# SyncE's transfers in written order, the maxima's split ahead of GpSimd's additions, and an opening with filters beside the loading of x

## The chip, the cores and the metric

The kernel runs on one core of one Trainium2 chip. Its time is device microseconds of that core; a verdict rests on the median of several executions. One execution was recorded by the hardware profiler, and the numbers that are read from a trace belong to that one. The engines are named as the profile names them: PE (TensorE), PEld (its weight loads), DVE (VectorE), ACT (ScalarE), POOL (GpSimd) and SP (SyncE, which issues transfers and computes nothing).

## What is computed

A block of a transformer on x of shape 4 x 2048 x 512, all in float32: a layer norm, then x + attention + a layer of experts. Attention has 16 heads of 32; queries and keys pass through a filter in the frequency domain, which is linear over the 32 numbers of a head and can therefore be multiplied into the weights. Cut to what matters:

```python
xn = _layernorm(x)                      # over 512, no scale or offset
q, k, v = split(xn @ w_qkv)             # 16 heads of 32
mask = sigmoid(mask_logits)
q = irfft(rfft(q) * mask); k = irfft(rfft(k) * mask)
attn = softmax(q k^T / sqrt(32))        # 2048 x 2048 for each of 4 x 16
attention = (attn v) @ w_out + b_out
best = argmax(softmax(xn @ w_gate))     # top 1 of 8 experts
# the first 100 tokens of each expert, in order of tokens, get
# gate * (xn @ w_expert + b_expert); all other tokens get 0
out = x + attention + experts
```

## The kernel before

**Groups, blocks and windows.** Four heads make a group; 4 sequences x 4 head groups make 16 groups `k`. A group has four blocks `n` of 512 queries. A block goes over the 2048 keys in 16 tiles `j` of 128 keys, two of them to a window, so a block has 8 windows, a group 32, and the program 512. In a window, for each tile and each pair of heads, TensorE first writes the negated row maxima into PSUM (`shift`, from the three bfloat16 rows of `negm`), adds the scores (`scores`), ScalarE takes the exponential into an `even` or `odd` tile, and one tile later TensorE multiplies with the values (`products`). For the sums of the softmax GpSimd adds each `odd` tile into its `even` one by an accumulating transfer (`pair`, line 834, 1 MB of traffic by the profile's count), and adds the `even` tiles up one window later (`add_to`).

**Maxima ahead of time.** The row maxima of a block are needed before its first exponential. A stream of items (`max_matmuls`, then `max_reduce` on VectorE) runs 40 items, that is ten windows, ahead. When a block is full, `max_negate` gives the negated maxima, and in the next window `max_close` (line 475) turns them with TensorE, ScalarE copies them out, GpSimd splits them into three bfloat16 rows, and SyncE sends these to `negm` (line 488).

**Closing a block.** `close_steps` (line 628) does, in windows after the block's end: 2 `fold` (row sums, to DRAM by SyncE, line 637), 3 `fetch` (back as 128 x 16, `few`, line 642), 4 `invert` (reciprocal on VectorE, and to DRAM), 5 `spread` (broadcast to `factor`), 7 `divide` on GpSimd (`ot`), 8 and 9 `result` (output projection, into `y`), 10 `add` (an accumulating transfer of 1 MB onto the output). The last block is closed by `close_last`, with a tile `y` read from the output before (line 888).

**Sequences.** While the third group of a sequence runs, the next sequence's x is loaded in four chunks (`load`, line 221), measured, given the bias and stored as the first sums of the output (`first_sums`, line 233); two chunks at a time fit. The chunks are loaded a second time, normalized and turned into `xnT` in the fourth group. `plan` (line 782) puts all such steps into windows: in the third group the loads of the four chunks at 11, 15, 19 and 23, the stores at 18, 22, 26 and 30, the second loads of the first two chunks at 30 and 31, the next weights (`load_qkv_weights`, line 381) at 31. The change of sequence is called a boundary here; there are three.

**What sets the order.** From line 724 on, TensorE, VectorE, ScalarE and GpSimd are wrapped in `InOrder`, which keeps the order in which the program writes their instructions. SyncE isn't wrapped: the framework's scheduler places its transfers where it expects them to be ready. Each engine then works its instructions off in that order, waiting for semaphores in place.

**The opening.** ScalarE issues the loads of the constants and of the weights (lines 128 to 181), SyncE those of x. The filter is made from the sigmoid (lines 182 to 188). For each of the four chunks of tokens the program measures, scales, normalizes and turns; after the first it filters group 0's weights (`filter_weights(0)`), writes them to DRAM (`wd`) and reads them back (`wg`). Two projections follow, then the first 40 items of maxima, with five further projections and the other three groups' filters between them. Then window 0 begins.

Of the kernel before, what the change touches and what calls it, by code (L numbers as in the profile page):

```python
# [22 lines left out]
H, DH = 16, 32  # L23
# [78 lines left out]
def attention_and_top1_experts(ctx: ExitStack, tc: tile.TileContext, a: dict, out: bass.AP):  # L102
# [24 lines left out]

    freq = const.tile([2 * NF, 2, P], F32, name="freq")
# [4 lines left out]
    falling = const.tile([P, E], F32, name="falling")  # L133
    nc.scalar.dma_start(out=falling, in_=a["c_falling"])
    token = const.tile([P, NT], F32, name="token")
    nc.scalar.dma_start(out=token, in_=a["c_token"])
    mask = const.tile([2 * NF, 1], F32, name="mask")
    logit_col = a["L0_attn_mask_logits"].rearrange("(f o) -> f o", o=1)
    nc.scalar.dma_start(out=mask[0:NF], in_=logit_col)
    nc.scalar.dma_start(out=mask[NF : 2 * NF], in_=logit_col)  # L140
# [30 lines left out]
    wd = [dram1.tile([P, NR, 3, P], F32, name=f"wd{c}") for c in range(NG)]  # L171
    raw = {}
    for s in range(2):
        for g in range(NR // 2):
            if g == 0:
                both = probs(s == 1)
            raw[s, g] = both[:, g]
            nc.scalar.dma_start(out=raw[s, g], in_=w_qkv[:, 2 * g : 2 * g + 2, s * DM : (s + 1) * DM])
    for c in range(NG):
        cols = slice(2 * DM + c * P, 2 * DM + (c + 1) * P)  # L180
        nc.scalar.dma_start(out=wd[c][:, :, 2, :], in_=w_qkv[:, :, cols])
# [9 lines left out]
    on = SimpleNamespace(tensor=nc.tensor, vector=nc.vector, scalar=nc.scalar, gpsimd=nc.gpsimd)  # L191
    def filter_weights(c):
        for s in range(2):
            pt, pw = bank(), bank()
            for r in range(NR):
                on.tensor.transpose(
                    pt[:, r * P : (r + 1) * P], raw[s, r // 2][:, r % 2, c * P : (c + 1) * P], ident
                )
            if s == 0:
                both = probs(c == 1)  # L200
            wt = both[:, s]
            on.scalar.copy(wt[:, 0, :], pt)
            for r in range(NR):
                at = slice(r * P, (r + 1) * P)
                on.tensor.matmul(pw[:, at], lhsT=wt[:, 0, at], rhs=filt, start=True, stop=True)
            on.scalar.copy(wt[:, 1, :], pw)
            nc.sync.dma_start(out=wd[c][:, :, s, :], in_=wt[:, 1, :].rearrange("p (r n) -> p r n", r=NR))
# [4 lines left out]
    def token_stage(b):  # L212
# [6 lines left out]
        def load(n, name="xs"):  # L219
            held[n] = chunk(name)  # L220
            nc.sync.dma_start(out=held[n], in_=x[b, n])
# [9 lines left out]
        def first_sums(n):  # L231

            nc.sync.dma_start(out=o[b, n], in_=held[n])

        def scale(first=0, last=NT):
            at = slice(first, last)
            on.scalar.activation(rstd[:, at], mv[:, at, 1], AF.Sqrt, bias=eps[:, 0:1])
            on.vector.reciprocal(rstd[:, at], rstd[:, at])
            on.gpsimd.tensor_tensor(shift[:, at], mv[:, at, 0], rstd[:, at], ALU.mult)
            on.gpsimd.tensor_scalar(shift[:, at], shift[:, at], -1.0, None, ALU.mult)  # L240
# [138 lines left out]
    wg, wo = {}, {}  # L379

    def load_qkv_weights(k):
        wg[k] = weights.tile([P, NR, 3, P], F32, name="wg", bufs=1)
        nc.sync.dma_start(out=wg[k], in_=wd[k % NG])

    def load_out_weights(k):
        c = k % NG
        wo[k] = weights.tile([P, DM], F32, name="wo")
        nc.sync.dma_start(out=wo[k], in_=a["L0_attn_w_out"][c * P : (c + 1) * P, :])
# [86 lines left out]
    def max_close(k, n):  # L475

        pn = bank()[0 : HG * TQ, 0:P]
        on.tensor.matmul(pn, lhsT=negs.pop((k, n)), rhs=ident, start=True, stop=True)
        rest = small.tile([HG * TQ, P], F32, name="rest")
        row = small.tile([HG * TQ, 3, P], BF16, name="row", bufs=2)  # L480
        on.scalar.copy(rest, pn)
        on.gpsimd.tensor_copy(row[:, 0, :], rest)
        for i in (1, 2):
            on.gpsimd.tensor_tensor(rest, rest, row[:, i - 1, :], ALU.subtract)
            on.gpsimd.tensor_copy(row[:, i, :], rest)
        negms[k, n] = qkv.tile([P, QB], BF16, tag="negm", name="negm", bufs=3)
        for i in range(3):
            nc.sync.dma_start(out=negms[k, n][i::DH, :], in_=row[:, i, :])
# [4 lines left out]
    def expert_steps():  # L493


        def begin():
            w_exp = chunk("w_exp")
            nc.sync.dma_start(out=w_exp, in_=a["L0_ffn_w_expert"].rearrange("(r p) n -> p r n", p=P))
            b_exp = work.tile([P, DM], F32, tag="b_exp", name="b_exp", bufs=1)
            nc.sync.dma_start(out=b_exp, in_=a["L0_ffn_b_expert"].partition_broadcast(P))  # L500
            entries = small.tile([P, NTAB, ST, 2], F32, name="entries")
            for i, table in enumerate(tables):
                nc.sync.dma_start(out=entries[:, i], in_=table.rearrange("(t p) c -> p t c", p=P))
# [124 lines left out]
    def close_steps(k, n, num, acc):  # L628
# [4 lines left out]
        def fold():  # L633
            den = work.tile([P, QB], F32, tag="den", name="den", bufs=1)
            on.scalar.copy(den, row_sums([acc]))
            held["sums"] = scratch.tile([HG, QB], F32, name="sums")
            nc.sync.dma_start(out=held["sums"], in_=den[0::DH, :])


        def fetch():  # L640
            held["few"] = small.tile([P, HG * QB // P], F32, name="few", bufs=2)
            nc.sync.dma_start(out=held["few"], in_=held["sums"].rearrange("h (c e) -> (h c) e", e=HG * QB // P))

        def invert():
            on.vector.reciprocal(held["few"], held["few"])
            held["inverse"] = scratch.tile([HG, QB], F32, name="inverse")
            nc.sync.dma_start(
                out=held["inverse"].rearrange("h (c e) -> (h c) e", e=HG * QB // P), in_=held["few"]
            )

        def spread():
            held["factor"] = work.tile([P, QB], F32, tag="factor", name="factor", bufs=1)
            for h in range(HG):
                nc.sync.dma_start(
                    out=held["factor"][DH * h : DH * (h + 1)], in_=held["inverse"][h].partition_broadcast(DH)
                )
# [12 lines left out]

        steps = [(2, fold), (3, fetch), (4, invert), (5, spread), (7, divide)]  # L670
        return steps + [(8, result, 0), (8, result, 1), (9, result, 2), (9, result, 3), (10, add)]

    def close_last(k, n, num, tiles, y):
# [9 lines left out]
        for t in range(TQ):  # L683
            on.vector.tensor_tensor(y[:, t, :], y[:, t, :], project(k, ot, t), ALU.add)
            if t % 2 == 1:
                nc.sync.dma_start(out=o[b, n, :, t - 1 : t + 1, :], in_=y[:, t - 1 : t + 1, :])
# [3 lines left out]
    for n in range(NQ):  # L690
        tiles = range(n * TQ, (n + 1) * TQ)
        load(n, "y" if n == 2 else "xs")
        for i in tiles:
            measure(i)
        scale(tiles[0], tiles[-1] + 1)
        for i in tiles:
            normalize(i)
            if i % 2 == 1:
                turn(i - 1)
        if n == 0:  # L700
            filter_weights(0)
            load_qkv_weights(0)
# [17 lines left out]
    first_projections = projections(0)  # L720
    for step in first_projections[:2]:
        step()
    ahead, first_projections = first_projections[2:7], first_projections[7:]
    on.tensor, on.vector, on.scalar, on.gpsimd = (
        InOrder(tc, engine) for engine in (nc.tensor, nc.vector, nc.scalar, nc.gpsimd)
    )
    closing = {}
    for i, item in enumerate(stream[:MAX_AHEAD]):
        if i % 4 == 0 and ahead:
            ahead.pop(0)()  # L730
        if i % 10 == 9 and i < 30:
            filter_weights(i // 10 + 1)
# [6 lines left out]
        max_reduce(item, half)  # L739
        while full_blocks:  # L740
            closing[i + 2] = full_blocks.pop(0)
            max_negate(*closing[i + 2])
        if i in closing:
            max_close(*closing[i])

# [36 lines left out]
    def plan(k):  # L782
# [18 lines left out]
        if k + 2 < B * NG:  # L801
            at(start + GW - 1, load_qkv_weights, k + 2)
# [3 lines left out]
        if c == NG - 2 and b + 1 < B:  # L806

            at(start + 10, begin_stage, b + 1)
            for n in range(NQ):
                at(start + 11 + 4 * n, in_stage, 0, n)  # L810
                at(start + 18 + 4 * n, in_stage, 7, n)
            for i in range(NT):
                at(start + 13 + i, in_stage, 1, i)
                at(start + 14 + i, in_stage, 6, i)
            at(start + GW - 2, in_stage, 2)
            at(start + GW - 2, in_stage, 0, 0)
            at(start + GW - 1, in_stage, 0, 1)
# [22 lines left out]
    pairs, adds = {}, {}  # L840
# [3 lines left out]
    for k in range(B * NG):  # L844
        plan(k)
        for n in range(NQ):
            num = work.tile([P, QB], F32, tag="num", name="num")
            tiles = {}
            for w in range(NW):
                even, odd = w * WIN, w * WIN + 1  # L850
                if window in pairs:
                    pair(*pairs.pop(window))
                if window in adds:
# [3 lines left out]
                for j in (even, odd):  # L857
# [14 lines left out]
                    while full_blocks:  # L872
                        block = full_blocks.pop(0)
                        max_negate(*block)
                        at(window + 1, max_close, *block)
                    if left:
                        products(*left)
                    left = k, n, j, tiles[j], num
                    for step in here[:cut] if j == even else here[cut:]:
# [6 lines left out]
                if last and w == NW - 2:  # L886
                    y = chunk("xs")
                    nc.sync.dma_start(out=y, in_=o[B - 1, n])
# [44 lines left out]
```

## Time and profile before

| | |
|---|---|
| median of 3 runs | 4551.49 us (4551.12 to 4552.34) |
| the profiled execution: time, span | 4547.31 us, 4545.5 us |
| PE, DVE, POOL, ACT busy, share of the span | 96%, 68%, 66%, 57% |
| mean granted clock of TensorE | 0.984 |
| transfers | 708.87 MB, 156 GB/s |
| transfers `even<-odd`, median from issue to landing | 8.1 us |
| `TENSOR_REDUCE part<-array` (maxima), mean | 1.10 us |
| `TENSOR_TENSOR even<-even` (additions), mean | 2.55 us |
| four groups of a sequence, from the first exponential | 285.8, 263.0, 279.2, 293.8 us (first sequence) |

The last row is read from ScalarE's timeline: four exponentials into `even` belong to a window, 32 windows to a group. PE and PEld overlap. Since a matmul's end is modelled, a busy PE is not yet PE at its peak; but where PE has no idle time between two instructions, nothing else bounds the stretch. A waiting instruction is shown with the time its engine was idle before it and what ended that, in square brackets. Instructions of the queues (SPq) are issues: the time given is that of the issue and not of the transfer.

### The profile page before, as it was taken

What the parts mean: (1) busy time and instruction counts of PE and PEld (TensorE: products, weight loads), DVE (VectorE), ACT (ScalarE), POOL (GpSimd) and SP (SyncE); (2) the same over time, 40 slices, a digit from 0 to 9 for tenths busy, and PEclk for the clock granted to TensorE, in tenths of its full rate; (3) what the DMA queues carried; (4) which work ended last, traced back from release to release, by engine and by line L of the source; (5) the groups of instructions that cost most, each with busy time, mean ns of one, the idle gap of its engine ahead of it and who ended that gap; (6) DMA issues with size and microseconds to landing.
All of it is one profiled execution on the core that took longest, in us unless ns stands there. A gap on an engine that the chain in (4) does not pass through costs nothing.

```text
span 4545.5 us, 106083 instructions
## 1 busy us (share of the span) xinstructions
PE 4381.8 (96%) x44390; PEld 1877.2 (41%) x44390; DVE 3099.6 (68%) x3609; ACT 2590.4 (57%) x4933; POOL 3002.4 (66%) x2082
## 2 busy tenths in 40 slices
PE   6999999989999999998999999998999999999997
PEld 3444443434434344443444434343343444434332
DVE  4666777765767777775667767776667766777772
ACT  3455565565555655556555555555655565555654
POOL 0477676755766766775577666776567665777666
PEclk9999999999999999999999999999999999999998
DMA  5587787877777878797677777788768776788787
GB/s 119 132 176 154 148 161 151 193 174 145 151 149 144 163 154 160 154 211 171 125 150 149 160 152 146 163 175 181 162 127 159 155 148 128 152 171 163 153 166 146
DMA packets 193231, 708.87 MB, mean 156 GB/s; under 512 B 47778, under 2 KB 54084, under 8 KB 127344
## 3 DMA queue, kind: packets, MB, share of 16 engines
q0 software_dynamic: 110576, 606.88, 68.4%
q1 hardware_dynamic: 77800, 91.56, 6.6%
q8 instruction: 347, 5.69, 0.5%
q10 hardware_dynamic: 4376, 3.67, 0.4%
q14 instruction: 132, 1.08, 0.1%
HBM read 77.09 MB, written 89.99 MB: 37 GB/s over the span
## 4 chain that ended last, share of the span: by engine, by line
PE 85%; DMA 7%; POOL 3%; issue 2%; ACT 2%; DVE 1%; ACTq 0%; POOLq 0%; SPq 0%; DVEq 0%
PE array L82 85%; DMA even<-odd 3%; POOL even L82 2%; DMA few<-sums 1%; DMA negm<-row 1%; ACT odd L82 1%; DMA sums<-den 1%; DVE part L82 1%; DMA wg<-wd 0%; POOL ot L82 0%; DMA wd<-in_L_attn_w_qkv_dram 0%; ACT even L82 0%; PE array L394 0%; POOL table L82 0%; ACT xs L82 0%
## 5 line engine op out<-in xcount | busy, mean ns | idle before, releaser
L82 DVE TENSOR_REDUCE part<-array 128x2 f32<-128x1024 f32 (+1 forms) x2308 | 2432.7, 1099 | 1222.0 <-PE array L82 1210.0
L82 POOL TENSOR_TENSOR even<-even 128x1024 f32<-128x1024 f32 x892 | 2171.4, 2549 | 236.0 <-DMA even<-odd 234.1
L82 PE MATMUL array<-k,q 32*128 32x512 f32 x8192 | 2228.0, 623 | 1.9 <-DVE part L82 1.9
L82 PE MATMUL array<-q,k 32*128 32x512 f32 x8192 | 2057.8, 596 | 0.0
L82 ACT ACTIVATE even<-array 128x512 f32<-128x512 f32 x2048 | 1065.5, 601 | 501.6 <-PE array L82 484.5
L82 ACT ACTIVATE odd<-array 128x512 f32<-128x512 f32 x2048 | 1060.3, 601 | 442.1 <-issue 236.6
L82 POOL DMA_DIRECT2D even<-odd x511 | 464.0, 908 | 1059.9 <-ACT odd L82 865.4
L82 PEld LDWEIGHTS array<-k,q 32*128 32x128 f32 x8192 | 811.1, 184 | 175.1 <-DVE num L82 74.1
L82 PE MATMUL array<-negm,ones_b 3*128 3x512 bf16 x4096 | 799.4, 383 | 53.0 <-DMA negm<-row 35.5
L82 PEld LDWEIGHTS array<-q,k 32*128 32x128 f32 x8192 | 751.2, 186 | 11.4 <-issue 2.5
L82 DVE TENSOR_TENSOR num<-num,array 128x512 f32<-128x512 f32 x960 | 650.5, 678 | 60.8 <-PE array L82 39.8
L82 PEld LDWEIGHTS <-ones_b 3*128 3x128 bf16 x4096 | 203.5, 92 | 934.0 <-issue 775.3
L82 PE MATMUL array<-even,v 128*32 128x512 f32 x4096 | 547.2, 606 | 15.5 <-ACT odd L82 15.4
L82 PE MATMUL array<-odd,v 128*32 128x512 f32 x4096 | 549.4, 607 | 3.1 <-ACT even L82 3.1
L82 PE MATMUL array<-xnT,wg 128*32 128x512 f32 x4032 | 456.7, 592 | 1.6 <-DVE part L82 1.0
L82 PE MATMUL array<-wo,ot 128*32 128x512 f32 x2048 | 260.1, 599 | 17.8 <-POOL ot L82 17.8
L82 PEld LDWEIGHTS array<-xnT,wg 128*32 128x32 f32 x4032 | 130.4, 110 | 300.9 <-issue 265.1
L82 PEld LDWEIGHTS array<-even,v 128*32 128x32 f32 x4096 | 80.8, 108 | 406.4 <-ACT odd L82 396.6
L82 PEld LDWEIGHTS array<-odd,v 128*32 128x32 f32 x4096 | 81.3, 108 | 399.5 <-ACT even L82 389.2
L82 PEld LDWEIGHTS array<-wg,xnT 128*32 128x32 f32 x8192 | 226.4, 110 | 40.4 <-issue 23.4
L82 ACT COPY y<-array 128x512 f32<-128x512 f32 x252 | 147.8, 587 | 162.7 <-PE array L82 162.6
L82 PE MATMUL array<-wg,xnT 128*32 128x128 f32 x8192 | 236.6, 273 | 0.9 <-issue 0.9
(141 smaller groups left out, 1366.2 us busy)
## 6 DMA issues: line engine op xcount, KB each, us to landing
even<-odd POOLq DMA_DIRECT2D x511, 1024.0 KB, 8.1
out_dram<-y POOLq DMA_DIRECT2D x63, 1024.0 KB, 12.7
xs<-in_L_attn_x_dram SPq DMA_DIRECT2D x31, 1024.0 KB
out_dram<-xs SPq DMA_DIRECT2D x16, 1024.0 KB
factor<-inverse SPq DMA_DIRECT2D x252, 64.0 KB
wg<-wd SPq DMA_DIRECT2D x16, 768.0 KB
wo<-in_L_attn_w_out_dram SPq DMA_DIRECT2D x16, 256.0 KB
negm<-row SPq DMA_DIRECT2D x192, 4.0 KB
```

What stands on the lines that cost most here:

```text
L82: done = act(*args, **kwargs)
```

## The change

It has four parts.

1. SyncE is wrapped in `InOrder` too, from the end of the opening on. Its transfers stand in written order. Together with it, steps of `plan` move: loads at 11, 15, 20 and 24, stores at 19, 23, 28 and 32, measures and biases of the second half one window later, the weights at 30, the second load of chunk 1 at 33.
2. `max_close` is done right after the first tile of its window, with ScalarE writing the first bfloat16 row itself. The other GpSimd operations and the transfers become `max_split`, one window later, after that window's `pair` and before its `add_to`.
3. The opening: SyncE loads the weights of queries and keys first, then all four chunks of x (the fourth into an `even` tile), then the weights of the values. All eight filter steps come first, half a step apart, with VectorE copying out the transposes; group 0's filtered weights stay in `wg`. The shift is one VectorE operation. The turns of chunks 1 to 3 go between the 40 items, in the place of the filters.
4. The last but one block of the program takes its reciprocal of the row sums on VectorE over 128 x 512 and closes in windows 2 to 6. The load of line 888 stands at its written place.

The core of the diff (plain renames of `nc.sync` to `on.sync` left out but for one):

```diff
-    on = SimpleNamespace(tensor=nc.tensor, vector=nc.vector, scalar=nc.scalar, gpsimd=nc.gpsimd)
-    def filter_weights(c):
...
+    on = SimpleNamespace(sync=nc.sync)
+    on.tensor, on.vector, on.scalar, on.gpsimd = (
+        InOrder(tc, engine) for engine in (nc.tensor, nc.vector, nc.scalar, nc.gpsimd)
+    )
+
+    def filter_steps(c):
+        held = {}
+        def turned(s):
+            if s == 0:
+                held["wt"] = probs(c % 2 == 1)
+            pt = bank()
             for r in range(NR):
                 on.tensor.transpose(
                     pt[:, r * P : (r + 1) * P], raw[s, r // 2][:, r % 2, c * P : (c + 1) * P], ident
                 )
+            on.vector.tensor_copy(held["wt"][:, s, 0, :], pt)
+        def filtered(s):
+            pw = bank()
+            wt = held["wt"][:, s]
             for r in range(NR):
                 at = slice(r * P, (r + 1) * P)
                 on.tensor.matmul(pw[:, at], lhsT=wt[:, 0, at], rhs=filt, start=True, stop=True)
+            done = pw.rearrange("p (r n) -> p r n", r=NR)
+            if c == 0:
+                on.scalar.copy(wg[0][:, :, s, :], done)
+            else:
+                on.scalar.copy(wt[:, 1, :], pw)
+                nc.sync.dma_start(out=wd[c][:, :, s, :], in_=wt[:, 1, :].rearrange("p (r n) -> p r n", r=NR))
+        return [lambda f=f, s=s: f(s) for s in range(2) for f in (turned, filtered)]
...
+            if shift_on:
+                shift_on.scalar_tensor_tensor(
+                    out=shift[:, at], in0=mv[:, at, 0], scalar=-1.0, in1=rstd[:, at], op0=ALU.mult, op1=ALU.mult
+                )
+                return
...
+        on.scalar.copy(row[:, 0, :], pn)
         on.scalar.copy(rest, pn)
-        on.gpsimd.tensor_copy(row[:, 0, :], rest)
+        closed[k, n] = rest, row
+
+    closed = {}
+
+    def max_split(k, n):
+        rest, row = closed.pop((k, n))
         for i in (1, 2):
             on.gpsimd.tensor_tensor(rest, rest, row[:, i - 1, :], ALU.subtract)
             on.gpsimd.tensor_copy(row[:, i, :], rest)
         negms[k, n] = qkv.tile([P, QB], BF16, tag="negm", name="negm", bufs=3)
         for i in range(3):
-            nc.sync.dma_start(out=negms[k, n][i::DH, :], in_=row[:, i, :])
+            on.sync.dma_start(out=negms[k, n][i::DH, :], in_=row[:, i, :])
...
+        def fold_here():
+            held["factor"] = work.tile([P, QB], F32, tag="factor", name="factor", bufs=1)
+            on.vector.reciprocal(held["factor"], row_sums([acc]))
...
+        if (k, n) == (B * NG - 1, NQ - 2):
+            return [(2, fold_here), (3, divide), (4, result, 0), (4, result, 1), (5, result, 2), (5, result, 3), (6, add)]
...
+    load(0)
+    load(1)
+    load(2, chunk("y"))
+    load(3, probs(False).rearrange("p u h q -> p (u h) q"))
...
+    filters = [filter_steps(c) for c in range(NG)]
+    turned, filtered = ([f[2 * s + i] for f in filters for s in range(2)] for i in range(2))
+    for i in range(2 * NG + 1):
+        if i < 2 * NG:
+            turned[i]()
+        if i > 0:
+            filtered[i - 1]()
+        if 2 * NG - TQ <= i < 2 * NG:
+            measure(i - 2 * NG + TQ)
+    nc.sync.dma_start(out=wd[0], in_=wg[0])
+    first_projections = projections(0)
+    scale(0, TQ, on.vector)
+    for i in range(TQ):
+        normalize(i)
+        measure(TQ + i)
+        if i % 2 == 1:
+            turn(i - 1)
...
+    ahead = {1: lambda: turn(4), 3: lambda: turn(6), 6: first_projections[2]}
+    ahead.update({9: lambda: turn(8), 11: lambda: turn(10), 14: first_projections[3]})
+    ahead.update({17: lambda: turn(12), 19: lambda: turn(14), 22: first_projections[4]})
+    ahead.update({28: first_projections[5], 33: first_projections[6]})
...
+    on.sync = InOrder(tc, nc.sync)
...
-            at(start + GW - 1, load_qkv_weights, k + 2)
+            at(start + GW - 2, load_qkv_weights, k + 2)
...
-            for n in range(NQ):
-                at(start + 11 + 4 * n, in_stage, 0, n)
-                at(start + 18 + 4 * n, in_stage, 7, n)
+            for n, (come, go) in enumerate(((11, 19), (15, 23), (20, 28), (24, GW))):
+                at(start + come, in_stage, 0, n)
+                at(start + go, in_stage, 7, n)
             for i in range(NT):
-                at(start + 13 + i, in_stage, 1, i)
-                at(start + 14 + i, in_stage, 6, i)
-            at(start + GW - 2, in_stage, 2)
+                at(start + 13 + i + i // 8, in_stage, 1, i)
+                at(start + 14 + i + i // 8, in_stage, 6, i)
+            at(start + GW - 1, in_stage, 2)
             at(start + GW - 2, in_stage, 0, 0)
-            at(start + GW - 1, in_stage, 0, 1)
+            at(start + GW + 1, in_stage, 0, 1)
...
                 if window in pairs:
                     pair(*pairs.pop(window))
+                if window in splits:
+                    max_split(*splits.pop(window))
                 if window in adds:
                     add_to(*adds.pop(window))
...
+                    if j == even and window in full:
+                        splits[window + 1] = full.pop(window)
+                        max_close(*splits[window + 1])
```

## The prediction

> **What bounds the kernel now.** I read the page's busy table and slices first, then the windows view over the stretches in which TensorE is not full, then the timelines of SyncE, TensorE, VectorE and GpSimd inside them.
>
> ```profile
> PE 4381.8 (96%) x44390; PEld 1877.2 (41%) x44390; DVE 3099.6 (68%) x3609; ACT 2590.4 (57%) x4933; POOL 3002.4 (66%) x2082
> PE   6999999989999999998999999998999999999997
> ```
>
> TensorE is the bound; no other engine passes 68%. The slices show where it isn't full: the first, three inside (each a boundary between two of the four sequences) and the last. The windows view prices them:
>
> ```profile
> 1512.00:1774.00 262.00, 262.00 (x2736) 111.89 (x2735) 189.42 (x214) 154.69 (x297) 176.14 (x118) 1.00 0.77 154
> 0.00:30.00 30.00, 8.04 (x31) 6.19 (x32) 9.21 (x27) 6.75 (x10) 1.35 (x13) 1.00 1.10 217
> 30.00:60.00 30.00, 22.09 (x130) 10.93 (x132) 3.35 (x11) 19.61 (x34) 1.23 (x6) 0.72 0.68 171
> 929.00:955.00 26.00, 13.06 (x106) 6.16 (x104) 10.95 (x15) 10.10 (x19) 19.90 (x18) 0.81 0.99 241
> 990.00:1002.00 12.00, 5.07 (x40) 2.59 (x42) 3.62 (x7) 3.18 (x7) 8.27 (x5) 0.76 0.87 188
> ```
>
> Columns: stretch, length, busy of PE, PEld, DVE, ACT, POOL, granted clock, DMA share, GB/s. The first row is an ordinary head group (32 windows of two key tiles): full, 262 us, so nothing is to be won there. The opening leaves 22 + 8 us of 60 idle, at a clock of 0.72 in its second half. The last two rows are the two holes of the first boundary. SyncE's timeline, with the lines of TensorE and VectorE that wait on it, says what they are:
>
> ```profile
> 930.24 0.40 SPq L233 DMA_DIRECT2D out_dram<-xs  x1
> 930.68 0.50 SPq L383 DMA_DIRECT2D wg<-wd  x1
> 934.70 0.38 SPq L221 DMA_DIRECT2D xs<-in_L_attn_x_dram  x1
> 937.75 2.79 SPq L488 DMA_DIRECT2D negm<-row  x3
> 951.81 0.61 PE L82 MATMUL array<-negm,ones_b 3*128 3x512 bf16 x2 [11.35 <-DMA negm<-row]
> ...
> 975.95 0.53 SPq L637 DMA_DIRECT2D sums<-den  x1
> 976.57 1.24 SPq L221 DMA_DIRECT2D xs<-in_L_attn_x_dram  x1
> 982.32 0.35 SPq L642 DMA_DIRECT2D few<-sums  x1
> 999.25 0.25 DVE L82 RECIPROCAL few<-few 128x16 f32<-128x16 f32 x1 [8.38 <-DMA few<-sums]
> ```
>
> Both holes are small transfers behind big ones: 12 KB of `negm` behind 2.8 MB issued within 5 us, and 8 KB of `few` behind 1 MB. In the first TensorE waits itself, in the second VectorE does, and TensorE then lacks free banks (6.93 us until "DVE part"). The tail has the same form:
>
> ```profile
> SPq L888 <- DMA out_dram<-y: 32.5, 1, 32.5
> 4362.54 0.41 SPq L888 DMA_DIRECT2D xs<-out_dram  x1
> 4363.03 1.26 SPq L637 DMA_DIRECT2D sums<-den  x1
> 4376.55 0.25 DVE L82 RECIPROCAL few<-few 128x16 f32<-128x16 f32 x1 [9.63 <-DMA few<-sums]
> 4495.33 0.25 DVE L82 RECIPROCAL few<-few 128x16 f32<-128x16 f32 x1 [10.17 <-DMA few<-sums]
> 4532.71 1.32 POOL L82 DMA_DIRECT2D out_dram<-y  x1 [3.99 <-ACT y L82]
> ```
>
> The load of line 888, wanted at the very end, sits early in SyncE's order and blocks it for 32.5 us; and the last thing issued is the accumulation of the last but one block, whose landing ends the span at 4545.5.
>
> **What the Trainium skill says.** "DMA: Bandwidth & Descriptors", section "Queues, rings and completion order": within a ring an engine consumes descriptors in order, and rows take turns by packet. The trace agrees: `negm`, issued by 940.5, serves at 951.8, with 2.8 MB ahead of it in SyncE's row. Its section "Anatomy of one DMA" adds that a semaphore wait happens on the issuing sequencer before dispatch; line 888 shows it, with `sums` coming out 0.5 us after it. "TensorE: Matmul & The Clock Gate", "Part 1: The HAM clock gate": after an idle window of about 3.4 us the clock is halved, and returns after one such busy window. The windows of 9 us show 0.50 at 946 to 955 and 0.98 after it; so a hole costs some 2 us more than its length.
>
> **The change, part by part.** Sums are made against the profiled span.
>
> *Opening.* In before the first exponential of window 0 starts at 126.2 (ScalarE's timeline), the first maximum at 64.76. The filter waits for the sigmoid, which stands behind ScalarE's own weight issues until 21.84; group 0's filtered weights go to DRAM and back (35.2 to 47.3). After: by the 5 MB that landed by 18.7, a MB takes 3.6 us; 2 MB of weights are in by about 9.5, the four x chunks by about 24. Eight filter rounds at 0.63 (4 transposes) + 1.16 (4 filter matmuls) = 1.8 on TensorE make 14.4, plus the last half round: end near 25. VectorE's copies and the four measures (0.66 + 0.16 each) lie beside them. Then table load 1.28, Sqrt 0.30, reciprocal and shift 0.4, gaps 0.5: 27.5. ScalarE's 4 normalizations (0.81) and 4 copies (0.59), 5.6, end at 33; two projections of 3.64 and a copy: 41. TensorE will have idled from 25 to 30, so I add 4 us of half clock: first maximum near 45. The 40 maxima are paced by VectorE: 40 x 1.16 = 46.4, and before took 61.4 until the exponential, 15 of them waits for TensorE: five projections (they stay, about 9) and three filters with their copies in between (about 6). In their place six turns of 1.2 us, without a round trip, about 2: 57. Window 0 then starts near 102, 24 us sooner; GpSimd's two shift operations per scale, 0.45, are in it. I take 22, between 14 (a cold clock through the rounds) and 30. The tables, now behind the filters on SyncE (12.6 us of issue), end before about 60; the first `negm` comes after 95.
>
> *SyncE in written order, with the loads and stores at new windows* (11, 15, 20, 24 and 19, 23, 28, 32; weights one window sooner, second chunk two later). Window starts are every fourth exponential into `even`. The group before a boundary takes 279, the ordinary one 262; windows 30 and 31 took 8.6 and 18.8 against 6.8 and 6.3, window 4 of the next group 15.6 against about 7.6, and some 3 us are spread out: 25 us per boundary. The rest by which the group after the boundary is longer is its own work and stays. After: at window 31 `negm` has weights and one chunk ahead, both issuable since window 29 because their slots are free; the store follows it. 1.8 MB at the 2.8 MB per 21 us seen here take 13.5 us, so they are through before window 32. `few` at 35 follows a load from 33. Both holes should close. What may open: at windows 11 and 19 `few` now stands directly behind a load and a store; nothing if the 10 us from few's issue to the reciprocal (579.4 to 589.8 in an ordinary group) suffice, 8.4 each as above if not: 0 to 50 us in all. I take 5 per boundary, since the accumulation of y starts about 10 us before there and not 4. Gain 3 x 20 = 60, between 15 and 75. No queued transfer waits long in the new order: behind a store waiting for GpSimd's bias stands `inverse` at most, and the bias is one window older. Experts' inputs (1.3 MB and the tables' entries) move from far ahead to two windows before use: 0 to 10 once, I take 0.
>
> *Maxima.* GpSimd's first cast (0.28) goes, ScalarE's copy (0.24) comes: 64 x 0.24 = 15 us on an engine 57% busy, hidden by TensorE. The four other operations move from behind the additions of their window to behind the next window's transfer issue (0.9); they come out about as late as before (602.55 then, after an addition that ended there), and the transfer 2 us sooner. The `neg` matmul comes half a window sooner. I take 0; from -6 in the tail, where windows take 4.4 to 7 us, to +5.
>
> *Tail.* Without line 888's block the hole at 4370 (7.9, and 2 of clock) goes: 9. The last but one block's reciprocal stays on chip: 128x512 at 0.85 per 128 columns is 3.4 of VectorE, which is idle there; TensorE's 6.2 us at 4490 go, but GpSimd was waiting until 4492.28 for its own transfer, so 4 count. Its result leaves at window 6: four projections (4 us) leave the end, and 4545.5 falls to the stores, issued by 4531.2 and about 4 us long. Against that, the 1 MB accumulation now contends with the last pair, whose landing the row sums need (8 to 14 us): 6 net. 19 in all, between 8 and 30.
>
> Sum: 22 + 60 + 0 + 19 = 101. Span 4545.5 to 4444.5; with the 1.8 us around it 4446.3. The profiled execution (4547.31) stood 4.2 under the median of the runs (4551.49); so the median goes to **4450.5**.
>
> **Rivals.** *The boundary stalls move.* The 50 us of new waits for `few`, or the second chunk (asked for one window before its normalization) holding ScalarE, eat most: 5 per boundary remain, 22 + 15 + 19 = 56: 4495. For it: DMA shares of 1.0 around boundaries, and as many bytes as before. Against: they are spread over more windows. *Everything closes*: 28 + 75 + 30 = 133: 4418. For it: no other engine is above 68%. Against: the tail is paced by the pairs (8.1 us to landing) and additions. *Slower: `negm` late at every block.* The split now waits behind a transfer that waits for the window's last exponential. In before the third `negm` issue ends 8 to 12 us before its block's first exponential, in the last block of a group 4 to 5; 1 to 2 of these go, and landing takes 2 to 3. It decides from (101 + 9) / 61 = 1.8 us lost per block; at 3 us, 183 lost: 4633. Against: only every fourth block is that near. *No effect*: SyncE's order in the built program does differ, so this is nearly excluded.
>
> **How the numbers follow.** Forecast 0.70, moved stalls 0.16, all closed 0.08, late `negm` 0.05, no effect 0.01. The bounds of the parts taken half together give 4412 to 4502, which takes in the first two rivals; left out are the slower case, no effect and the forecast's own outer tails. A measurement of this kernel can tell about 0.2% from no change. Faster 0.94, same 0.01, slower 0.05.
>
> **What would show it.** Opening: first exponential near 102, TensorE's second 30 us filled. Boundaries: the waits on `negm` and on `few` gone from TensorE and VectorE, groups 2 and 3 about 10 us shorter each; if I am wrong, VectorE waits on `few` in windows 12 and 20 of group 2. Tail: no wait of SyncE on `out_dram<-y`, the span ended by stores. Ordinary groups still 262; at 265 or more, the late `negm` holds. Any time above 4502 means that it or moved stalls dominate.

## The result, and the profile after

The changed kernel takes 4535.64 us (median of 8, 4523.94 to 4546.23) where the kernel before takes 4552.34 (median of 8, 4545.89 to 4560.1) on the same chip: a ratio of 0.9963, 95% interval 0.9949 to 0.9977. That is 17 us or 0.37% faster. The forecast was 101 us, and the time lies outside the range.

The profiled execution took 4531.95 us. First its page: the span, the busy times, TensorE's slices, and the row of the matmuls that read `negm` (busy, mean ns | idle before, and what ended most of it).

```profile
span 4530.2 us, 106235 instructions
PE 4390.8 (97%) x44390; PEld 1881.8 (42%) x44390; DVE 3113.0 (69%) x3626; ACT 2597.8 (57%) x4988; POOL 2956.7 (65%) x2010
PE   8999999999999999999999999999999999999997
L82 PE MATMUL array<-negm,ones_b 3*128 3x512 bf16 x4096 | 797.2, 384 | 78.4 <-DMA negm<-row 69.9
```

The opening has filled (first digit 8 where there was a 6), and the three slices inside that showed the boundaries stand at 9 like their neighbours. The last row is the surprise: TensorE now waits 69.9 us for `negm`, against 35.5 in the kernel before, although both holes at the boundaries were to close. Two rows of the list of waits (us in total, times, longest), first before and then after, and the windows view after say that they nearly did:

```profile
DVE few L82 <- DMA few<-sums: 63.6, 13, 10.2
...
PE array L82 <- DMA negm<-row: 35.5, 5, 11.4
```

```profile
PE array L82 <- DMA negm<-row: 69.9, 22, 7.5
```

```profile
DVE few L82 <- DMA few<-sums: 4.8, 3, 2.3
```

```profile
1491.10:1758.10 267.00, 263.16 (x2734) 112.58 (x2732) 189.13 (x214) 155.26 (x300) 173.66 (x113) 0.99 0.76 151
0.00:30.00 30.00, 17.15 (x109) 15.71 (x110) 12.28 (x28) 11.86 (x18) 0.90 (x11) 0.90 0.96 323
30.00:60.00 30.00, 28.59 (x191) 11.26 (x189) 20.83 (x37) 16.48 (x29) 0.00 (x0) 0.87 0.43 29
913.80:932.40 18.60, 13.27 (x116) 4.93 (x110) 13.25 (x16) 11.65 (x21) 14.69 (x15) 0.99 1.01 249
958.00:968.00 10.00, 10.00 (x92) 4.45 (x89) 8.30 (x9) 8.77 (x17) 5.58 (x3) 1.00 1.07 204
```

VectorE waited 63.6 us for `few` in 13 places before, now 4.8 in 3. The last row is the stretch in which the hole of `few` was: TensorE is full. In the row before it, windows 30 and 31 ahead of the boundary, 5.3 us are still idle (in the stretch shown of before it was 12.9). The first row is the ordinary group that took 262.0 us with TensorE full. It now takes 267 and has 3.8 us of idle time. Such a hole is in the last window of *every* group that another follows: 15 of the 22 waits, 48.0 of the 69.9 us. Before there were 5 waits.

By kind, from the first exponential of each group (the rows add up to the span):

| us | before | after | forecast of the difference |
|---|---|---|---|
| until the first exponential | 126.2 | 99.9 (-26.3) | -22 |
| nine groups away from the boundaries, called ordinary (0, 1, 4, 5, 8, 9, 12, 13, 14) | 2423.2 | 2471.9 (+48.7) | 0 |
| six groups at the three boundaries | 1722.6 | 1694.3 (-28.3) | -60 |
| the last group, to the end | 273.5 | 264.0 (-9.5) | -19 |

The end looks as expected: SyncE waits for `out_dram<-y` nowhere, and the last thing issued is the stores:

```profile
4524.76 1.86 SPq L82 DMA_DIRECT2D out_dram<-xs  x2
```

### The profile page after: what moved, and what is told of

Same layout as the page of the kernel before. It is cut to its first block, busy times and chain, and to the rows that moved or that the text cites. A ratio compares the mean times of both kernels' runs of the same rounds, so it can differ in the third digit from the quotient of the medians.

```text
span 4530.2 us, 106235 instructions
## 1 busy us (share of the span) xinstructions
PE 4390.8 (97%) x44390; PEld 1881.8 (42%) x44390; DVE 3113.0 (69%) x3626; ACT 2597.8 (57%) x4988; POOL 2956.7 (65%) x2010
## 3 DMA queue, kind: packets, MB, share of 16 engines
q14 instruction: 135, 1.11, 0.1%
## 5 line engine op out<-in xcount | busy, mean ns | idle before, releaser
L82 POOL DMA_DIRECT2D even<-odd x511 | 443.5, 868 | 1194.9 <-ACT odd L82 1014.6
L82 PE MATMUL array<-negm,ones_b 3*128 3x512 bf16 x4096 | 797.2, 384 | 78.4 <-DMA negm<-row 69.9
L82 PE MATMUL array<-xnT,wg 128*32 128x512 f32 x4096 | 465.8, 595 | 1.7 <-DMA wg<-wd 1.0
```

Of the source, the lines that this page charges most:

```text
L82: done = act(*args, **kwargs)
```

## The experiments

**Where the new wait comes from.** Here is the end of the same group, the tenth, in both kernels: GpSimd's last cast of the split, its pair transfer, SyncE's issue of `negm`, and TensorE's matmul that waits. First before:

```profile
2865.11 2.21 SPq L488 DMA_DIRECT2D negm<-row  x3
...
2866.49 0.28 POOL L82 CAST row<-rest 16x128 bf16<-16x128 f32 x1
2866.99 0.88 POOL L82 DMA_DIRECT2D even<-odd  x1 [0.21 <-issue]
```

Then after:

```profile
2850.69 4.00 SPq L82 DMA_DIRECT2D negm<-row  x3
2851.61 0.86 POOL L82 DMA_DIRECT2D even<-odd  x1 [1.25 <-ACT odd L82]
...
2853.52 0.28 POOL L82 CAST row<-rest 16x128 bf16<-16x128 f32 x1
...
2861.06 0.61 PE L82 MATMUL array<-negm,ones_b 3*128 3x512 bf16 x2 [3.69 <-DMA negm<-row]
```

The three issues of `negm` are shown as one line; the third starts at 2866.80 before and at 2853.82 after. Before, the pair goes out 0.2 us *after* it; after, 2.2 us *ahead*. The packet records of the DMA queues show the rest: the 256-byte packets of `negm` end 1.29 us after the third issue in the median block before, and 4.89 us after. Two theories were set against each other. A: the split behind the pair makes `negm` late. B: SyncE's written order (the weights' load in window 30, other transfers in front) does.

**split_first** takes only the order of two calls back:

```diff
-                if window in pairs:
-                    pair(*pairs.pop(window))
                 if window in splits:
                     max_split(*splits.pop(window))
+                if window in pairs:
+                    pair(*pairs.pop(window))
```

> One swap in the changed kernel: the split of the maxima stands ahead of the window's pair transfer and not behind it; SyncE's order, the plan's windows, the opening and the tail stay. Theory A (the split behind the pair makes negm late): the 256-byte packets of negm end about 1.5 us after the third issue instead of 4.4 to 5.0, window 31 of the groups falls from 8.0-11.9 us (12.8 to 13.0 at the boundaries) to 6.3-6.6, ordinary groups from 267-272 to 262-264, TensorE's waits on negm from 69.9 us to under 10, the median 4460 to 4480. Theory B (it is SyncE's written order, with the weights load in window 30 and the bookkeeping transfers ahead of negm): ordinary groups stay at 266 or more, waits on negm above 50 us, the median within 12 us of the changed kernel's 4536.

4462.38 us, ratio to before 0.9809 (0.9786 to 0.9832). Packets end 1.29 us after the issue, window 31 takes 6.3 (8.0 at the boundaries), the waits on `negm` are 3.8 us, ordinary groups 261.5 to 266.4 apart from the three that are longer in before too (0, 12 and 13). Theory A holds, with group 14 at 266.4 and the windows 31 of the boundaries at 8.0 a little out. This swap alone gives 70 us. The same place in its trace:

```profile
2807.76 1.88 SPq L82 DMA_DIRECT2D negm<-row  x3
...
2808.69 0.28 POOL L82 CAST row<-rest 16x128 bf16<-16x128 f32 x1
2809.18 0.88 POOL L82 DMA_DIRECT2D even<-odd  x1 [0.21 <-issue]
```

The weights' load is in front of `negm` here too (SyncE issues `wg` at 2806.42), and it does no harm in this place: `negm`'s matmuls don't wait.

**old_close** undoes all of part 2 (close and split as one step of the next window's agenda, behind the additions, the first cast on GpSimd).

```diff
...
-                        full[window + 1] = filled
+                        at(window + 1, max_close, *filled)
+                        at(window + 1, max_split, *filled)
...
```

> The second part of the change undone: close and split of the maxima as one step of the next window's agenda, behind the additions, all four GpSimd operations and the first cast on GpSimd; SyncE's written order, the plan's windows, the opening and the tail of the changed kernel stay. Theory A: negm's packets end 1.3 to 2 us after the third issue, ordinary groups 262 to 264, window 31 at 6.3 to 6.6 (up to 9 at the boundaries), the median 4460 to 4485. Theory B: ordinary groups 266 or more, the median within 12 us of 4536.

4466.0 us, 0.9813 (0.979 to 0.9835); packets 1.29 us after the issue; ordinary groups 261.9 to 264.7 with the same exceptions. So part 2 as written costs 1.5%, and put ahead of the pair it brings nothing that can be told from its old place. Moving the split ahead of the *additions* brought nothing that these runs can tell; moving it behind the *transfer* was the loss.

**last_cast** asks what of the pair is in the way: GpSimd's time, or the bytes.

```diff
             on.gpsimd.tensor_tensor(rest, rest, row[:, i - 1, :], ALU.subtract)
+            if i == 2:
+                yield
             on.gpsimd.tensor_copy(row[:, i, :], rest)
...
+                split = max_split(*splits.pop(window)) if window in splits else iter(())
+                next(split, None)
                 if window in pairs:
                     pair(*pairs.pop(window))
-                if window in splits:
-                    max_split(*splits.pop(window))
+                next(split, None)
```

> As split_first, but the last of the split's four GpSimd operations (the cast of the third row, 0.3 us) stands behind the pair transfer's issue; the other three stay ahead of it. It parts two forms of theory A. A1, GpSimd's own work behind the pair is what is late (some 1.5 us of subtractions and casts): negm's third issue comes 1.4 us sooner than in the changed kernel, and most of the gain of split_first stays, 4465 to 4490. A2, the packets of negm share the DMA engines with the 1 MB pair that was issued just ahead: they still end 4 us or more after the third issue, TensorE's waits on negm stay above 45 us, window 31 above 7.5 us, and the median is 4510 to 4535. Theory B: as split_first, near 4536.

4540.67 us, 0.9981 (0.9972 to 0.999). The waits on `negm`, 64.9 us, and the windows 31, 8.6 us or more, are as A2 has them; the time is 6 us above its range. So 0.36 us of GpSimd's work behind the pair lose the whole gain. Its trace at the same place:

```profile
2857.07 2.42 SPq L82 DMA_DIRECT2D negm<-row  x3
2858.02 0.88 POOL L82 DMA_DIRECT2D even<-odd  x1
2858.58 0.36 POOL L82 CAST row<-rest 16x128 bf16<-16x128 f32 x1
...
2866.54 0.39 PE L82 MATMUL array<-negm,ones_b 3*128 3x512 bf16 x2 [2.81 <-DMA negm<-row]
```

The third issue comes 0.95 us after the pair's, the packets end 5.87 us after it, 6.8 after the pair. In the changed kernel it is 2.2 + 4.9 = 7.1. Behind the pair, the moment at which `negm` is issued hardly matters: it lands when the pair is through.

**half_pairs** and **half_ahead** ask how the engines divide their time. The pair is 128 elements of 8 KB, eight for each of 16 DMA engines if they share them evenly, 0.64 us each.

```diff
-        on.gpsimd.dma_start(out=first, in_=second, accum_op=ALU.add)
+        for u in range(2):
+            on.gpsimd.dma_start(out=first[:, u], in_=second[:, u], accum_op=ALU.add)
```

> The changed kernel, split behind the pair as it is, but each pair goes as two accumulating transfers of half the size, one for each half of the tile. In the changed kernel the pair's elements start 1.4 us after its issue and end at 7.4, and the packets of the third negm row come at 5.9 to 7.1, that is behind nearly all of it. C1, an engine takes a whole transfer's share (eight elements) from one row before it turns to the other: behind halves negm goes after the first half, its packets end within 2.5 us of the third issue instead of 4.9, TensorE's waits on negm fall from 69.9 us to 30 or less, the median is 4480 to 4510 (GpSimd issues twice, about 0.9 us more per window). C2, what was issued earlier goes first, whatever its division: negm still ends more than 4 us after the third issue, waits stay above 55 us, the median is 4525 or more.

4515.71 us, 0.9922 (0.9906 to 0.9939): between the two in time. Packets end 4.21 us after the third issue and the waits are 62.3 us: both signs in the trace are C2's, the time is below C2's 4525. The waits are 7.6 us shorter where the time is some 19 us shorter; where the rest comes from is open. Of `negm`'s packets that come behind the pair, about a third passes between 4.5 and 6 us after the first half's issue, the rest as both halves end.

```diff
-    def pair(first, second):
-        on.gpsimd.dma_start(out=first, in_=second, accum_op=ALU.add)
+    def pair(first, second, us=(0, 1)):
+        for u in us:
+            on.gpsimd.dma_start(out=first[:, u], in_=second[:, u], accum_op=ALU.add)
...
                 if window in pairs:
-                    pair(*pairs.pop(window))
+                    pair(*pairs[window], (0,))
                 if window in splits:
                     max_split(*splits.pop(window))
+                if window in pairs:
+                    pair(*pairs.pop(window), (1,))
```

> As half_pairs, but only the first half of the pair is issued ahead of the split, the second half behind the split's last operation. D1, negm's packets wait for the elements that are ahead of them on their engines, and the halves of half_pairs were both ahead: the first half's elements end about 4 us after its issue, the third issue comes at 2.3 to 2.5, so negm ends 2 to 3 us after the third issue, TensorE's waits on negm are 20 to 45 us, the median 4480 to 4505. D2, any accumulating transfer in flight keeps them out until it is through: 4.2 us or more after the third issue, waits 60 us or more, 4512 to 4530.

4468.93 us, 0.9829 (0.9812 to 0.9846), better than either theory had it. The waits (34.8 us) are in D1's range, the landing (3.80 us after the third issue) is between the two. The landing counts the slowest packet; in the median block half of the packets behind the third issue start within 2.2 us of it. With half the bytes ahead the stall in window 31 shrinks from 4.4 to 1.4 us, so the amount ahead counts. The exact rule by which an engine turns from one queue to the other isn't settled by these two.

The median over ten last windows of groups away from the boundaries, in us from that window's start (packet records for the landing):

| | pair issued | third `negm` issue | `negm` landed | window takes |
|---|---|---|---|---|
| before | 1.16 | 1.24 | 2.53 | 6.31 |
| split_first | 1.11 | 0.92 | 2.85 | 6.28 |
| half_ahead (first half) | -0.70 | 1.51 | 5.66 | 7.71 |
| last_cast | 0.46 | 1.42 | 7.37 | 10.08 |
| after | -0.68 | 1.55 | 7.72 | 10.71 |

The other windows in which a block closes are mostly 9.8 us long, since they hold a projection. There `negm` lands at 6.4 in the changed kernel and mostly no one waits. The last window of a group, 6.3 us without a projection, is too short. The fifteen last windows that another group follows take 59 us longer than in split_first, of the 72 us by which the two spans differ. The other seven waits, 21.9 us together, stand in windows 7, 15 and 23, where blocks close too.

**What SyncE's written order is worth.** Two kernels leave it out, one on the changed kernel, one on split_first.

```diff
-    on.sync = InOrder(tc, nc.sync)
```

> The changed kernel without SyncE in written order: the framework's scheduler places its transfers again, all else stays, the split behind the pair too. Theory A: ordinary groups stay at 266 to 272 and window 31 at 8 us or more, since the pair is still ahead of negm; the boundary waits come back in part (VectorE on few above 15 us), the load of the last y blocks SyncE again, so the median is 4545 to 4580. Theory B: ordinary groups go back to 262-264, TensorE's waits on negm in ordinary groups go, the median is 4490 to 4520.

> Split ahead of the pair, as in split_first, and SyncE's order left to the scheduler. If the written order is worth by itself what the difference of unordered and the changed kernel says (4590 to 4536), it is 4505 to 4525, with the holes at windows 29 to 31 of groups 2, 6 and 10 back (15 us or more in one of them) and ordinary groups at 262 to 264. If the scheduler's order only hurt because negm was already late, it is 4462 to 4475.

| ratio to before | split behind the pair | split ahead of it |
|---|---|---|
| written order | 0.9963 (0.9949 to 0.9977) | 0.9809 (0.9786 to 0.9832) |
| scheduler's order | 1.0091 (1.0067 to 1.0115) | 0.9943 (0.9927 to 0.996) |

The medians are 4590.21 us for unordered, above the range of theory A, and 4524.49 for first_unordered, at the upper edge of its first reading. In unordered, windows 31 are at 8.0 us or more, as A has it, but three of the six ordinary groups are below its 266 (263.4 to 264.9). Down a column the order is worth 1.3% in both, 58 and 61 us; along a row the split is worth 1.5% in both. Within the intervals the two add up. Without the order the changed kernel is *slower* than before, and its trace has the old holes back: VectorE waits 56.6 us for `few`, SyncE is blocked by the last `y` again, and at the boundary a load of x slips between the rows of `negm`:

```profile
SPq L951 <- DMA out_dram<-y: 34.7, 1, 34.7
```

```profile
927.23 0.40 SPq L242 DMA_DIRECT2D out_dram<-xs  x1
927.73 0.54 SPq L509 DMA_DIRECT2D negm<-row  x1
931.63 0.38 SPq L230 DMA_DIRECT2D xs<-in_L_attn_x_dram  x1
932.12 2.60 SPq L509 DMA_DIRECT2D negm<-row  x2
```

**first_oldplan**: split_first with the windows of loads, stores, measures and weights as in the kernel before.

```diff
-            at(start + GW - 2, load_qkv_weights, k + 2)
+            at(start + GW - 1, load_qkv_weights, k + 2)
...
-            for n, (come, go) in enumerate(((11, 19), (15, 23), (20, 28), (24, GW))):
-                at(start + come, in_stage, 0, n)
-                at(start + go, in_stage, 7, n)
+            for n in range(NQ):
+                at(start + 11 + 4 * n, in_stage, 0, n)
+                at(start + 18 + 4 * n, in_stage, 7, n)
...
```

> As split_first, SyncE in written order, but loads, stores, measures and the next weights in the windows of the kernel before. If the new windows carry the boundaries' gain, negm of the next group's first block stands in SyncE's order behind the weights, a load and a store that waits for its bias: window 31 of groups 2, 6 and 10 at 12 us or more, boundary groups 5 to 12 us longer each, 4480 to 4505 in all. If the written order alone carries it, 4462 with 8 to either side.

4453.34 us, 0.9783 (0.9767 to 0.98), not slower than split_first. The new windows bring nothing; the written order carries the boundaries alone. My expectation had the queue wrong. An agenda step of window 31 stands behind that window's split, so `negm` goes ahead of the weights:

```profile
903.65 4.92 SPq L82 DMA_DIRECT2D negm<-row  x3
908.67 0.41 SPq L82 DMA_DIRECT2D wg<-wd  x1
909.18 0.82 SPq L82 DMA_DIRECT2D xs<-in_L_attn_x_dram  x1
```

**first_oldtail**: split_first with the last but one block closed like all others.

```diff
-        if (k, n) == (B * NG - 1, NQ - 2):
-            return [(2, fold_here), (3, divide), (4, result, 0), (4, result, 1), (5, result, 2), (5, result, 3), (6, add)]
```

> As split_first, but the last but one block is closed like all others (row sums to DRAM, back, reciprocal of 128 x 16, broadcast; result in windows 8 and 9, its accumulation at 10). My sum gave this part of the tail about 10 us: 4468 to 4478, the span ended again by the landing of the accumulation of y, 10 us or more after the last store's issue. If the row sums' pairs pace the tail, nothing: 4462 with 4 to either side.

4477.42 us, 0.9835 (0.9818 to 0.9852). In the traces the stretch from the last group's start is 271.5 us against 259.5: 12 us for this part, and the accumulation of `y`, issued at 4465.87, ends the span again. The runs' intervals overlap narrowly, so the size is the traces', and it is rough: with the changed tail that stretch took from 251.5 us (half_ahead) to 268.1 (old_close).

**opening_only**: the kernel before with the new opening, parts 1, 2 and 4 undone.

```diff
-    on.sync = InOrder(tc, nc.sync)
...
-                        full[window + 1] = filled
+                        at(window + 1, max_close, *filled)
+                        at(window + 1, max_split, *filled)
...
-            at(start + GW - 2, load_qkv_weights, k + 2)
+            at(start + GW - 1, load_qkv_weights, k + 2)
...
```

> The kernel before with the new opening alone: SyncE unordered, old windows, old close and split of the maxima, old tail. If the opening's gain lies where the trace of the changed kernel has it (first exponential 26 us sooner) and nothing later takes it back, the first exponential is at 98 to 102 and the median 24 to 30 us under before, 4520 to 4526 where before is at 4550. If the first groups give it back (tables and filtered weights landing later, as group 0 of the changed kernel was 5 us longer), it is 4535 or more.

4532.03 us, 0.9957 (0.994 to 0.9973), 12 to 27 us by the interval; the median lies between the two readings. The first exponential starts at 99.9, 26.3 sooner, but the span is only 15.3 shorter. The rest goes in pieces of 2 to 3 us, in groups 3, 12, 13 and 15. What takes it there wasn't found.

**first_divide_oldplan**, a version from these readings: first_oldplan with the division of a block's result ahead of its window's additions, since TensorE still waits 19.1 us for `ot` there.

```diff
+                for step in ahead_of_adds.pop(window, ()):
+                    step()
                 if window in adds:
                     add_to(*adds.pop(window))
...
-                    at(window + after, *step)
+                    if after == 7:
+                        ahead_of_adds[window + after] = step
+                    else:
+                        at(window + after, *step)
```

> A version from the readings so far: the split ahead of the pair, SyncE in written order, the windows of the kernel before, and the division of a block's result (ot) ahead of its window's additions on GpSimd and not behind them. In first_oldplan TensorE still waits 19 us for ot. If that wait sets the time, it goes to under 5 us and the median is 15 to 20 us under first_oldplan's 4453, 4433 to 4440. If the additions, which come 1.3 us later in that window, give it back, 4448 to 4458.

4446.87 us, 0.9769 (0.9753 to 0.9785), the fastest of all, 2.3% under before, and between the two readings. Against first_oldplan the intervals overlap. Its list of waits suggests why little came of it:

```profile
PE array L82 <- DVE part L82: 16.2, 7, 6.3
...
PE array L82 <- POOL ot L82: 6.8, 2, 5.2
```

The wait for `ot` fell by 12 us, and that for VectorE's maxima rose by 7 (9.0 in first_oldplan).

## Why the prediction was wrong

*The step that failed* is the maxima's: "they come out about as late as before (602.55 then, after an addition that ended there), and the transfer 2 us sooner. ... I take 0; from -6 in the tail, where windows take 4.4 to 7 us, to +5." Both observations hold: in a group's last window the third issue moved from 1.24 to 1.55 us, the pair from 1.16 to -0.68. The conclusion doesn't. The pair "2 us sooner" was counted as harmless, and it put 1 MB in front of 12 KB on the DMA engines. It cost 70 us instead of 0. With the split ahead of the pair the same kernel takes 4462.38, inside the range and 12 us from the forecast. That closeness owes something to errors that cancel: in its trace the opening gives 28.2 us (22 forecast), the boundaries 51.4 (60), the tail 14.0 (19), and the ordinary groups take 5.8 back.

The means to see it were in the text. The holes at the boundaries were read as "small transfers behind big ones", and the same rule wasn't asked of the transfer that the edit itself moved in front. From the Trainium skill, "DMA: Bandwidth & Descriptors", section "Queues, rings and completion order", I took only that rows take turns by packet. The section says that an engine drains a whole packet, about 9 to 17 descriptors typically, before it switches. The pair's eight elements on an engine come near the lower figure if each is one descriptor, which no run here shows. The trace of the changed kernel fits it: the pair's elements run from 1.4 to 7.4 us after its issue, and the first of `negm`'s packets behind the third issue starts at 5.9 in the median block. half_pairs shows that halving the transfers doesn't halve the wait, so this reading isn't the whole rule.

*The slower rival* had the right victim: `negm` late at every block, from 1.8 us per block on, at a chance of 0.05. Its objection, "only every fourth block is that near", was mostly right, and turned it into a cost of some 4 us once in a group. That was a case between forecast and rival which I had not priced. "Landing takes 2 to 3" was the mis-sized term: 4.9 us to the end of the packets in the median block, about 6 in a group's last.

*Opening.* Forecast 22, with 24 by the sum. The first exponential came 26.3 sooner, and alone the opening is worth 12 to 27. Right.

*Boundaries.* 60 forecast, 28.3 measured in the changed kernel, 51.4 in split_first; the difference is mostly the late `negm`: the windows 31 of these groups are 20.7 us longer in the changed kernel. Right in mechanism (`few`: 63.6 to 4.8 us of VectorE's waits; without the written order these groups take 56.5 us longer than in split_first), somewhat large in size. The new windows, on which the argument leans, brought nothing.

*Tail.* 19 forecast; 9.5 measured, 14.0 with the split ahead. The changed kernel's tail has waits on `negm` of its own in windows 7 and 23 of the last group, 4.8 and 7.5 us of TensorE (before: 3.3 us, in window 23). The last but one block's own close gave some 12 where the sum had 10.

*"At 265 or more, the late `negm` holds"* was the sign named beforehand, and it is the one that showed: 267 to 272 in six of the ordinary groups. "Any time above 4502 means that it or moved stalls dominate" came true as well.

*The range* does not follow from the parts as written: all their bounds together give some 4410 to 4520, half the way to each some 4430 to 4485. The measured time lies outside all of these.

## What to carry to other kernels

When an edit moves an instruction past a transfer, ask what that transfer will now stand in front of on the DMA engines, and not only how much time its issuing engine gains. In this kernel the small transfer that someone waits for belongs ahead of the large one, though they are in different queues: 0.36 us of work on the wrong side cost as much as the whole split. And price a wait at the place with the least slack: most blocks absorbed it here, and the last of each group paid some 4 us.

## What was unexpected of the hardware

Here two queues of different engines were not independent: 12 KB on SyncE's queue landed 1.29 us after the issue with the pair behind it, 4.89 with the pair 2.2 us ahead, and 5.87 with it 0.95 us ahead, so the time of landing followed the pair's and not the issue's. Dividing that pair into two transfers that are both ahead made it only 0.7 us shorter; moving one half behind, 1.1.
